# Layer 0 of a two-layer transformer block: the attention scores of two query blocks issued together

## The chip, the cores and the metric

The kernel runs on one core of one Trainium2 chip. The time is the device time of one execution in microseconds, and the median of three runs is compared. All tensors are float32. TensorE (PE) does matmuls and transposes and loads weights beside them (PEld); VectorE (DVE), ScalarE (ACT) and GpSimd (POOL) do the rest; SyncE (SP) issues most DMAs. Matmul results go to PSUM, which has eight banks of 512 float32 values on each of 128 partitions.

## The reference, cut to what matters

Two post-norm layers follow each other: causal attention with 32 heads of 16 dimensions and 8 key/value heads, then a linear layer with dequantized weights; attention with heads of 128 dimensions and a distance bias, then a linear layer with ternary weights. Only the first attention is touched by the change. Four sequences (batches) of 256 tokens:

```
q = (x @ Wq + bq).reshape(B, S, 32, 16).transpose(0, 2, 1, 3)
k = (x @ Wk + bk).reshape(B, S, 8, 16).transpose(0, 2, 1, 3)
v = (x @ Wv + bv).reshape(B, S, 8, 16).transpose(0, 2, 1, 3)
...
scores = jnp.einsum('bhqd,bhkd->bhqk', q, k) / jnp.sqrt(16.)
scores = jnp.where(causal, scores, NEG)
p = jax.nn.softmax(scores, axis=-1)
out = jnp.einsum('bhqk,bhkd->bhqd', p, v)
...
x = _layernorm(x + out @ Wo + bo)
```

## The kernel before, in words

The attention of layer 0 is a loop of 64 steps (L584 to L594): batch b (0 to 3), query tile qt (0 or 1, 128 tokens each), parity e of the key/value head (0 or 1), and block n (0 to 3) of 32 queries. A step is one call of `begin0`. Its four score matmuls (L502) take the four key/value heads of one parity, one in each quarter of 32 rows of the PE array; a block's four query heads times 32 queries are the 128 columns of the weights, and the keys are streamed. Causality lets a step stop at w = 128 qt + 32 (n + 1) keys, so the width runs over 32, 64, 96 and 128 in the first tile and 160, 192, 224 and 256 in the second. Each matmul writes its own bank: the tile `sc` has four banks, and its pool `ps_s0` holds one such tile. The other four banks are three for everything else (`ps_w`) and one for the attention's result `o`.

DVE adds the mask and moves the scores to SBUF in one instruction (L505: pr <- sc, causal), which is what frees the four banks. It takes the maximum (L511: nm); ACT does four exponentials with their sums (L289); DVE takes the reciprocal of the sums of the block before (L294, in `divided`, kept in program order), and POOL multiplies by it (L297). Six `pr` buffers rotate. Four steps later `transpose0` turns the probabilities on PE (L535: pt), and ACT or DVE copies them to `prT0` (L107, L105: prT). After the fourth block of a parity `end0` multiplies by v (L551: o). After both parities `o` is copied to `oT`, and a generator `tail0` for that 128-token tile starts: py = oT @ Wo (L458), residual and statistics (y L460, L272 to L274), a power on POOL (rs L275), normalisation (x L279), four transposes (pt_x L285), a copy to x1T (L107), the second matmul pf (L475), again norm, transposes and a copy to x2T. `fill` advances these tails and the projections of the next batch (`project0`: pk L401, pq L414, pv L434) by one piece a step.

The order in which instructions stand on an engine is not written out by hand: the tile framework reorders the program by its own estimates, apart from instructions that are kept in program order. Each engine runs its list in order, so an instruction that waits holds up everything behind it. In the second tile most copies of prT, and the copy of oT, are ACT's, in the same list as the exponentials (L566 gives the second tile's copies to ACT).

The norm of batch b, tile qt is called with tt = 2 b + qt. Where the text says "batch 1, pf to py", it means pf of tile tt = 1, whose matmuls run while batch 1 is in the attention, and py of tt = 2.

Of the kernel before, what the change touches and what calls it, by code (L numbers as in the profile page):

```python
# [12 lines left out]
F32 = mybir.dt.float32  # L13
# [7 lines left out]
P = 128  # L21
# [43 lines left out]
def block_kernel(  # L65
# [20 lines left out]
    nc = tc.nc  # L86

    def pool(stack, name, bufs=1, **kw):
        return stack.enter_context(tc.tile_pool(name=name, bufs=bufs, **kw))
# [42 lines left out]
    for g in range(G - 1):  # L132
        rows = slice(32 * g, 32 * g + 32)
# [8 lines left out]
    ps_s0 = pool(la, "ps_s0", 1, space=PSUM)  # L142
# [145 lines left out]
    def exponentials(pr, sc, nm, sums, i, w):  # L288
        nc.scalar.activation(  # L289
            pr[:, i, 0:w], sc, AF.Exp, bias=nm[:, i : i + 1], accum_out=sums[:, i : i + 1]  # L290
        )
# [9 lines left out]
    def softmax_tiles(sp, name, bufs, room=True):  # L301
        nm = sp.tile([P, G], F32, tag="nm", name=f"nm_{name}", bufs=bufs + 2)
        sums = sp.tile([P, G], F32, tag="sums", name=f"sums_{name}", bufs=bufs + 2)
        pr = sp.tile([P, G, 2 * P], F32, tag="pr", name=f"pr_{name}", bufs=bufs) if room else None
        return nm, sums, pr
# [69 lines left out]
    qkv0 = {}  # L375
# [114 lines left out]

    ahead, tails = deque(), deque()

    def begin0(b, qt, e, n):

        qT, kT, _ = qkv0[b]
        w = qt * P + 32 * (n + 1)
        name = f"0_{b}_{qt}_{e}_{n}"
        nm, sums, pr = softmax_tiles(a0, name, 6)
        sc = ps_s0.tile([P, 4, 4 * P], F32, tag="s", name=f"sc_{name}")
        for r in range(4):  # L500
            rows = slice(32 * r, 32 * r + 32)
            nc.tensor.matmul(  # L502
                sc[:, r, 0:w], qT[rows, 4 * qt + n].rearrange("p i q -> p (i q)"), kT[rows, e, 0:w], start=True, stop=True
            )
        nc.vector.tensor_tensor(  # L505
            pr[:, :, 0:w],
            sc[:, :, 0:w],
            causal[:, 2 * P - w :].unsqueeze(1).to_broadcast([P, G, w]),
            ALU.add,
        )  # L510
        nc.vector.tensor_reduce(nm, pr[:, :, 0:w], AX.X, ALU.max, negate=True)  # L511
        for r in range(4):
            exponentials(pr, pr[:, r, 0:w], nm, sums, r, w)
        divide0()
        undivided.append((pr, sums, w))
        return pr

    open0 = {}
    undivided = []

    def divide0():


        if undivided:
            divided(*undivided.pop(), True)
# [52 lines left out]
    def fill():  # L578
# [5 lines left out]
    run(  # L584
        [(b, qt, e, n) for b in range(B) for qt in range(2) for e in range(2) for n in range(4)],
        begin0,
        transpose0,
        end0,
# [543 lines left out]
```

## Time and profile before

| | us |
|---|---|
| median of three runs (936.08 to 938.96) | 937.45 |
| the profiled execution | 938.1 |
| its span, first to last instruction | 936.3 |
| PE busy | 894.2 (95%) |
| DVE busy | 600.0 (64%) |
| POOL busy | 427.8 (46%) |
| ACT busy | 315.6 (34%) |
| the attention of layer 0 with its tails, from the trace | about 20 to 250 |

The first row is what is compared. The profiled execution is one more execution, with 1.8 us outside its span. A busy share is of the whole span, and the two layers differ: ACT is far busier in layer 0 than its 34% says. A row of a timeline gives start, duration, engine, line, what is written and read, the shape, how many records it merges, and in brackets the idle time before it and what ended it. A matmul of float32 leaves two records, a transpose one. Stretches are given as A:B, with length, then busy time and instructions of PE, PEld, DVE, ACT and POOL, then the granted PE clock, the DMA share and GB/s.

### The profile page before, as it was taken

How to read it: one execution, taken by the hardware profiler on the slowest of the kernel's cores; microseconds unless marked ns; L12 is line 12 of the kernel's file. 1: busy time of each engine (PE TensorE's matmuls, PEld its weight loads, DVE VectorE, ACT ScalarE, POOL GpSimd, SP SyncE). 2: the span in 40 equal slices, each digit the busy share in tenths (PEclk: the TensorE clock that was granted, in tenths of full speed). 3: DMA queues.
4: the chain of work that ended last, by engine and by line, in shares of the span. 5: the costliest groups of instructions: out<-in, count | busy, mean ns of one | idle time of the engine just before them, and what ended most of it. 6: DMA issues, size and time to landing. Idle time of an engine off the chain costs nothing.

```text
span 936.3 us, 12053 instructions
## 1 busy us (share of the span) xinstructions
PE 894.2 (95%) x3849; PEld 549.0 (59%) x3849; DVE 600.0 (64%) x1393; ACT 315.6 (34%) x1220; POOL 427.8 (46%) x470
## 2 busy tenths in 40 slices
PE   7989999998999998999999999999999999999995
PEld 6655565554444445666666666666666666667552
DVE  2867867868324457555676676666676666666575
ACT  1675675668410012222212222122221121214341
POOL 4443543435355124336434634543553534657732
PEclk9999999999999999999999999999999999999998
DMA  9500000000110104434443544353444433432001
GB/s 251 186 1 1 1 2 1 1 1 1 44 48 22 45 1 105 121 102 142 106 134 82 134 134 113 112 135 93 122 123 113 121 84 111 135 90 71 1 34 57
DMA packets 76421, 74.49 MB, mean 80 GB/s; under 512 B 5957, under 2 KB 52678, under 8 KB 76358
## 3 DMA queue, kind: packets, MB, share of 16 engines
q1 hardware_dynamic: 75014, 72.02, 27.0%
q10 hardware_dynamic: 1344, 1.70, 0.6%
q8 instruction: 31, 0.51, 0.2%
q14 instruction: 32, 0.26, 0.1%
HBM read 49.58 MB, written 24.12 MB: 79 GB/s over the span
## 4 chain that ended last, share of the span: by engine, by line
PE 80%; POOL 7%; DVE 7%; ACT 3%; issue 1%; DMA 1%; ACTq 0%; POOLq 0%; DVEq 0%
PE p_q L658 19%; PE po L911 15%; PE o L1037 8%; PE sc L999 7%; PE p_k L658 5%; PE p_v L658 5%; PE py L458 3%; PE pf L475 3%; PE py L868 3%; PE pq L414 2%; PE pt L535 2%; ACT pr L289 2%; PE o L551 2%; PE sc L502 2%; POOL pr L297 1%; DVE pr L505 1%
## 5 line engine op out<-in xcount | busy, mean ns | idle before, releaser
L297 POOL TENSOR_TENSOR pr<-pr,sums 128x512 f32<-128x512 f32 (+7 forms) x128 | 168.6, 1318 | 230.7 <-DVE sums L294 214.3
L289 ACT ACTIVATE pr<-sc,nm 128x32 f32<-128x32 f32 (+7 forms) x256 | 95.0, 378 | 236.3 <-DVE nm L1015 214.3
L289 ACT ACTIVATE pr<-pr,nm 128x32 f32<-128x32 f32 (+7 forms) x256 | 102.9, 403 | 45.8 <-DVE sums L294 28.2
L1007 DVE SCALAR_TENSOR_TENSOR sc<-table,sc 128x224 f32<-128x224 f32 (+7 forms) x256 | 87.7, 364 | 27.5 <-PE sc L999 25.7
L999 PEld LDWEIGHTS sc<-kT,qT 128*128 128x128 f32 x512 | 77.1, 191 | 32.6 <-issue 29.2
L1037 PE MATMUL o<-prT,v 128*128 128x512 f32 x192 | 92.9, 592 | 0.0
L672 DVE TENSOR_TENSOR qT<-p_q,qT 128x512 f32<-128x512 f32 x96 | 64.8, 687 | 37.3 <-PE p_q L658 37.3
L999 PE MATMUL sc<-kT,qT 128*128 128x160 f32 (+7 forms) x512 | 84.9, 307 | 1.9 <-ACT pr L289 1.9
L1015 DVE TENSOR_REDUCE nm<-sc 128x1 f32<-128x224 f32 (+7 forms) x256 | 71.3, 300 | 2.7
L323 DVE STREAM_TRANSPOSE blocks<-pr 128x512 f32<-128x512 f32 x84 | 57.3, 697 | 24.4 <-POOL pr L297 24.3
L911 PE MATMUL po<-wo,so 128*128 128x256 f32 x224 | 57.9, 381 | 2.6 <-POOL so L635 2.6
L658 PE MATMUL p_q<-x2T,ws_q 128*128 128x512 f32 x128 | 59.8, 592 | 0.0
L658 PE MATMUL p_q<-xt,ws_q 128*128 128x512 f32 x128 | 58.1, 595 | 0.0
L658 PE MATMUL p_q<-x2T,wq 128*128 128x512 f32 x128 | 57.6, 592 | 0.0
L107 ACT COPY o<-o 128x512 f32<-128x512 f32 x29 | 17.0, 585 | 120.4 <-PE o L1037 120.4
L911 PE MATMUL po<-wo,o 128*128 128x256 f32 x224 | 57.5, 379 | 0.0
L911 PE MATMUL po<-to,so 128*128 128x256 f32 x224 | 54.7, 388 | 0.9 <-POOL so L638 0.9
L107 ACT COPY prT<-pt 128x512 f32<-128x512 f32 (+2 forms) x82 | 44.4, 579 | 33.0 <-PE pt L535 28.7
L505 DVE TENSOR_TENSOR pr<-sc,causal 128x128 f32<-128x128 f32 (+3 forms) x64 | 47.6, 744 | 12.4 <-PE sc L502 11.6
L535 PE MATMUL pt<-ident,pr 128*128 128x128 f32 (+3 forms) x384 | 53.1, 275 | 2.2 <-ACT prT L107 1.9
L924 DVE TENSOR_TENSOR kept<-po,kept 128x512 f32<-128x512 f32 x48 | 33.1, 689 | 31.6 <-PE po L911 31.6
L911 PEld LDWEIGHTS po<-to,so 128*128 128x128 f32 x224 | 42.9, 193 | 16.6 <-issue 9.1
(165 smaller groups left out, 1541.6 us busy)
## 6 DMA issues: line engine op xcount, KB each, us to landing
way<-blocks SPq DMA_DIRECT2D x112, 128.0 KB, 2.5
prT<-way SPq DMA_DIRECT2D x28, 512.0 KB, 3.7
wq<-in_L_attn_w_qkv_dram SPq DMA_DIRECT2D x8, 1024.0 KB, 5.2
wo<-in_L_attn_w_o_dram SPq DMA_DIRECT2D x8, 1024.0 KB, 5.3
way<-blocks SPq DMA_DIRECT2D x112, 64.0 KB, 1.8
prT<-way SPq DMA_DIRECT2D x28, 256.0 KB, 2.6
wk<-in_L_attn_w_qkv_dram SPq DMA_DIRECT2D x4, 512.0 KB, 3.8
wv<-in_L_attn_w_qkv_dram SPq DMA_DIRECT2D x2, 1024.0 KB, 6.2
```

Source lines behind the costliest of these rows:

```text
L107: nc.scalar.copy(dst, src)
L289: nc.scalar.activation(pr[:, i, 0:w], sc, AF.Exp, bias=nm[:, i : i + 1], accum_out=sums[:, i : i + 1])
L297: nc.gpsimd.tensor_tensor(pr[:, :, 0:w], pr[:, :, 0:w], sums.unsqueeze(2).to_broadcast([P, G, w]), ALU.mult)
L323: nc.vector.transpose(blocks[:, kt].rearrange("p j h q -> p h j q"), pr[:, :, ts(kt, P)].rearrange("p h (j k) -> p h j k", k=32),)
L535: nc.tensor.transpose(pt[0:w, r, :], pr[:, r, kt * P : kt * P + w], ident)
L658: nc.tensor.matmul(bank, fixed, moving, start=(c == 0), stop=(c == 1))
L672: add = lambda dst, a, b: nc.vector.tensor_tensor(dst, a, b, ALU.add)
L911: nc.tensor.matmul(bank[:, ts(n, HALF)], left[:, c, :], right[:, c, :], start=(c == 0), stop=(c == 1),)
L999: nc.tensor.matmul(sc[:, m, 0:w], qT[:, 8 * b + 4 * qt + n].rearrange("p i q -> p (i q)"), kT[:, b * S : b * S + w], start=True, stop=True,)
L1007: nc.vector.scalar_tensor_tensor(sc[:, m, 0:w], table[:, 2 * P - w : 2 * P], table[:, 2 * P + kv : 2 * P + kv + 1], sc[:, m, 0:w], ALU.mul ...
L1015: nc.vector.tensor_reduce(nm[:, n : n + 1], sc[:, m, 0:w], AX.X, ALU.max, negate=True)
L1037: nc.tensor.matmul(o, v1[:, 2 * b + kt, ts(kv, P)], prT[:, kt].rearrange("p h n q -> p (h n q)"), start=(kt == 0), stop=(kt == qt),)
```

## The change

A new function `scores0` computes the scores of two neighbouring blocks, n and n + 1, when n is even, into one `sc` tile of the same four banks: each bank (512 values) is cut into two halves of 256, one a block. `begin0` calls it at even n only, keeps the tile in `open0`, and takes its half of it at every step. The number of matmuls, their shapes and the number of all other instructions stay as they are; the tile `sc` now comes free when the mask adds of both blocks have read it.

```diff
+    def scores0(b, qt, e, n):
+
+        qT, kT, _ = qkv0[b]
+        sc = ps_s0.tile([P, 4, 2, 2 * P], F32, tag="s", name=f"sc_0_{b}_{qt}_{e}_{n}")
+        for m in range(2):
+            w = qt * P + 32 * (n + m + 1)
+            for r in range(4):
+                rows = slice(32 * r, 32 * r + 32)
+                nc.tensor.matmul(
+                    sc[:, r, m, 0:w],
+                    qT[rows, 4 * qt + n + m].rearrange("p i q -> p (i q)"),
+                    kT[rows, e, 0:w],
+                    start=True,
+                    stop=True,
+                )
+        return sc
+
     def begin0(b, qt, e, n):
 
-        qT, kT, _ = qkv0[b]
         w = qt * P + 32 * (n + 1)
         name = f"0_{b}_{qt}_{e}_{n}"
         nm, sums, pr = softmax_tiles(a0, name, 6)
-        sc = ps_s0.tile([P, 4, 4 * P], F32, tag="s", name=f"sc_{name}")
-        for r in range(4):
-            rows = slice(32 * r, 32 * r + 32)
-            nc.tensor.matmul(
-                sc[:, r, 0:w], qT[rows, 4 * qt + n].rearrange("p i q -> p (i q)"), kT[rows, e, 0:w], start=True, stop=True
-            )
+        if n % 2 == 0:
+            open0["sc"] = scores0(b, qt, e, n)
+        sc = open0["sc"][:, :, n % 2]
         nc.vector.tensor_tensor(
             pr[:, :, 0:w],
             sc[:, :, 0:w],
```

## The prediction

> **What bounds the kernel now.** I read the page first, then busy time by stretches, the timeline of the first layer engine by engine, the waits of the score matmuls, and last the granted clock window by window. The change touches layer 0's attention alone (20 to 250 us), so the table by stretches matters most. Its columns are PE, PEld, DVE, ACT and POOL busy, PEclk, DMA share, GB/s; the cuts are batch ends, roughly.
>
> ```profile
> 20.00:60.00 40.00, 34.37 (x291) 24.56 (x290) 31.98 (x65) 30.10 (x127) 17.33 (x16) 1.00 0.38 131
> 60.00:118.00 58.00, 54.14 (x359) 32.26 (x357) 42.94 (x83) 35.25 (x141) 25.50 (x25) 0.97 0.00 1
> 118.00:177.00 59.00, 55.94 (x384) 34.35 (x384) 43.70 (x88) 37.09 (x149) 25.59 (x26) 1.00 0.00 1
> 177.00:229.00 52.00, 47.99 (x337) 26.38 (x338) 40.43 (x81) 36.79 (x149) 22.27 (x22) 1.00 0.01 1
> ```
>
> PE is busy 92 to 95% of three of the four, so it is the usual bound. But DVE and ACT have 60 to 80%, and PE's idle time is not spread: it stands before a few matmuls that wait for the softmax. The waits say which:
>
> ```profile
> L502 PE MATMUL sc<-kT,qT x512: 270/333/479, 21.3 to 233.5; 32*128 32x32 f32 x22, 32*128 32x128 f32 x22, 32*128 32x192 f32 x22, 32*128 32x64 f32 x21
> its engine sat idle before it (us, times) until:
>   DVE pr L505: 25.3, 32
> ...
>   DVE pr L505: 11.6, 15
> ```
>
> The first 25.3 us is PE (and its weight loader, counted beside it) waiting for the mask add L505 to free the four banks; the 11.6 us is DVE waiting for scores. Next the place that decides the sum, batch 1, second query tile (timeline of PE, then ACT):
>
> ```profile
> 111.06 0.55 PE L502 MATMUL sc<-kT,qT 32*128 32x160 f32 x8
> ...
> 113.84 0.61 PE L502 MATMUL sc<-kT,qT 32*128 32x192 f32 x8 [1.09 <-DVE pr L505]
> ...
> 116.28 0.66 PE L502 MATMUL sc<-kT,qT 32*128 32x224 f32 x8
> 117.97 1.55 PE L458 MATMUL py<-wop,oT 128*128 128x512 f32 x3 [1.02 <-ACT oT L107]
> ...
> 116.39 1.04 ACT L107 COPY prT<-pt 128x512 f32<-128x512 f32 x2
> 117.33 0.58 ACT L107 COPY oT<-o 128x512 f32<-128x512 f32 x1
> 117.81 0.46 ACT L289 ACTIVATE pr<-pr,nm 128x192 f32<-128x192 f32 x1
> ```
>
> PE sits twice: for L505, and for ACT's copy oT, which stands behind one block's exponentials. Last, the clock around the two worst PE waits:
>
> ```profile
> 56.86:60.27 3.41, 1.67 (x12) 0.68 (x10) 2.26 (x3) 3.38 (x13) 1.02 (x2) 1.00 0.02 5
> 60.27:63.69 3.42, 3.42 (x6) 1.36 (x5) 0.00 (x0) 1.34 (x6) 1.00 (x1) 0.50 0.00 0
> 111.47:114.89 3.42, 2.33 (x28) 1.75 (x23) 3.29 (x5) 1.50 (x4) 1.32 (x3) 1.00 0.00 0
> 114.89:118.30 3.41, 2.39 (x22) 0.97 (x20) 3.03 (x5) 3.41 (x14) 3.12 (x2) 1.00 0.01 2
> ```
>
> A window with PE busy 1.67 of 3.41 us is followed by one at half clock; 2.33 and 2.39 are not punished (nor 1.91 at 855.6 us). 1.70 at 370.9 is. So the point lies at about 1.7 us idle, and one half-clock window costs up to 1.7 us of PE work.
>
> **The Trainium skill.** "TensorEngine Tiling (Array Packing)", Key Properties: changing the tiling mode drains TensorE. The trace agrees, priced below. "TensorE: Matmul & The Clock Gate", Part 1: the clock halves after an idle window of 3413 ns that runs free. The trace has this length, but half a window idle is enough. "PSUM — Partial Sum Buffer", section "PSUM bank collisions raise a hardware error": TensorE may not write a bank that another engine reads. So the first add cannot start while the second block's scores enter the same banks; no run here shows that case.
>
> **What a switch costs.** Scores use a quarter of the rows each (32*128), transposes the whole array. Transposes follow each other every 0.109 us, from row 132.49 in the timeline of 120 to 134 us: 12 take 1.46 to the next start, of which the first is 0.06 and the last 0.09 us too long. Between them a score group takes 0.35 us at width 32 and 0.64 at 256 (126.36 to 126.72, 124.26 to 124.90). So one w=256 group costs 0.79 with both edges; merged behind another it adds only its two streams, 2 x 0.215 (py: eight 512-column matmuls in 3.44 us, half of it for 256): 0.36 saved. At width 32/64 weight loads of 0.107 show and 0.29 is saved. The instruction orders give 68 runs of score matmuls before and 37 after (five pairs are split), and 157 changes of mode against 102. 31 runs x 0.33 = 10 us, which I use as 0.17 per saved change, 55 of them, 9.4 us. Matmul count, DMAs, SP's order and all of layer 1's order are the same, so nothing else is removed.
>
> **What moves.** (1) Scores of block n+1 are issued a step early, and the wait for L505 comes once per pair. (2) On DVE both adds now stand ahead of the first maximum: the first block's exponentials start one add later (0.81 to 1.21 us; row 128x768 is 0.93). (3) On ACT's order, in the second tile of batches 1, 2, 3, oT stands behind the exponentials of two blocks instead of one, and the x1T copy that pf needs likewise. A block of 192 is 4 x 0.445 = 1.78 us. (4) The added self-waits of PE name matmuls 9 or more back (once 5), which are over: nothing; if not, 0.1 us each (an edge as above), 22 of them. (5) POOL has the power that the norm needs behind one division more (up to 1.7 us) at the end of first tiles; L297 is done by then because the exponentials are earlier; else 1.7 us, where PE has other work.
>
> **The sum**, as lead (-) or lag (+) against the profiled run at the matmuls py and pf:
> - Batch 0, to py (59.67): ACT is busy from 41 us on and sets the end. It loses about 0.8 us waiting for the late maximum, gains 0.6 from earlier scores: +0.2.
> - To pf of tile 1 (105.27): of the waits of 1.7 us at 72.94, 75, 76 and 88, 1.5 go, since the adds are through before; with 8 changes (1.3 us) and 0.5 waiting for x1T, -2.1.
> - Batch 1, pf to py: now 12.70 us. After: +0.93 (second add) +1.78 (second exponentials) -0.94 (the two prT copies leave this chain): 14.4. -2.1 + 1.7 = -0.4. PE's own work there (pf 3.44, pq 1.7, 20 transposes 2.2, o 1.1, two score pairs 2.0) is 10.5 us: it idles 3.9 us in one piece, over the 1.7 point wherever the window falls. Half clock: +1.4 (0.7 to 1.7 by phase): +1.0.
> - Batch 2: 13 changes, -2.2, and the waits at 157.89 and 146.47, -1.1: -2.3; then again +1.7 and +1.4: +0.8.
> - Batch 3, to pf (216.16): 8 changes and a wait of 0.3, -1.7: -0.9 at py; its chain is 14.3 (3.7 from py to y, 4.0 statistics and norm, 1.7 two adds, 0.8 maximum, 3.45 two exponentials, 0.6 x1T) against 12.1: +2.2, so +1.3. Clock on pf itself +1.4: +2.7.
> - pf to py (228.65): 13.7 (3.6 to y, 3.6 to the norm, 1.7 adds, 0.8 maximum, 3.4 exponentials, 0.6 oT) against 12.5, +1.2; then 2.1 back, since the last block's scores are already done (0.9), the division before 240.59 is early (0.9) and two changes go (0.3); half clock once more +1.4: 3.2.
> From 250 us on nothing differs. The profiled execution took 938.1 us (span 936.3), 0.65 above the median 937.45. 937.45 + 3.2 is 940.7; I say 940.8, 0.36% slower. What measures apart from no change is about 0.3%, 2.8 us.
>
> **Rivals.** (A) Faster: the oT and x1T delays find cover, PE's waits before py stay under 1.7 us, no window halves. It then keeps the 9.4 us, less some 1 us at batch 0: about 929. For: PE is busy over 92%. Against: ACT's order puts eight exponentials before oT, and no PE work is left there. It decides at an idle of 1.7 us per window: below it, this; above, mine. With half of the chain's delay, 933. (B) Chains as computed, but the clock holds: four times 1.4 us less, 935.1, no change. Against: both half-idle windows of the trace were punished. (C) Larger stalls: DVE's reciprocals wait for exponentials in program order, so each delay blocks the adds behind them, a further 1 us per second tile and one more halving: 946. (D) The change does nothing, as all scores wait for the same adds: 937.5; the order, with 31 runs fewer, speaks against it.
>
> **Numbers.** Mine 0.46 (938.5 to 944), C 0.08, A 0.30, B 0.13, D 0.03. Mine falls partly within 0.3% (0.05). Faster 0.31, same 0.2, slower 0.49. The range leaves out the best of A and the worst of C: 929.5 to 945.5. Both signs hold much; the likeliest case's own range is 938.5 to 944.
>
> **What would show it.** Right: score rows x16, L505 mean unchanged, PE waiting for scores under 8 us against 25.3; PE idle of 3 us or more before py in batches 1 to 3 <-ACT oT; more than one window at 0.50 between 60 and 250 us. Wrong: oT waits under 1.5 us (A), or clock at 1.00 throughout (B); a wait for L505 over 2 us at each pair (C).

## The result and the profile after

The changed kernel takes 945.13 us (median of five runs, 942.64 to 947.94), the kernel before 936.32 in the same comparison. The ratio is 1.0096 (95% interval 1.0081 to 1.0111): 8.8 us slower. The direction was forecast, the size was not: 3.3 us were expected. The profiled execution of the changed kernel is its longest run, 947.94 us with a span of 946.1, against 938.1 and 936.3 before; its excess of 9.8 us is the one taken apart here. Below, py_2 is the py of tile tt = 2, and so on.

The same four stretches as before the change (length, then busy time of PE, PEld, DVE, ACT, POOL, granted clock):

```profile
20.00:60.00 40.00, 33.30 (x295) 25.18 (x294) 32.99 (x67) 31.09 (x132) 18.62 (x16) 0.96 0.41 132
60.00:118.00 58.00, 53.22 (x365) 32.58 (x364) 41.17 (x83) 35.37 (x144) 24.77 (x25) 0.97 0.00 1
118.00:177.00 59.00, 54.22 (x384) 34.52 (x383) 43.63 (x88) 37.16 (x149) 25.87 (x25) 0.97 0.01 2
177.00:229.00 52.00, 45.81 (x332) 26.59 (x335) 36.35 (x77) 32.92 (x131) 19.77 (x20) 0.94 0.00 1
```

PE is busy less in every stretch, and yet gets no further: its clock, 1.00 in three of the four before, is now 0.94 to 0.97 in all. A busy share that falls can mean that work was saved or that the engine waits; here it is both. What the score matmuls wait for (the waits of their line, 502 before, 501 now):

```profile
L501 PE MATMUL sc<-kT,qT x512: 270/318/478, 21.5 to 229.0; 32*128 32x64 f32 x22, 32*128 32x128 f32 x22, 32*128 32x192 f32 x22, 32*128 32x32 f32 x21
...
  DVE pr L518: 8.6, 8
...
  DVE pr L518: 9.9, 7
```

PE's wait for the mask add fell from 25.3 us in 32 places to 8.6 in 8, and DVE's wait for scores from 11.6 to 9.9. The change does what it says (the forecast had put the first wait under 8). Now the place shown before, batch 1, second tile (timeline of PE, then of ACT):

```profile
112.46 1.09 PE L501 MATMUL sc<-kT,qT 32*128 32x224 f32 x16
117.19 2.66 PE L458 MATMUL py<-wop,oT 128*128 128x512 f32 x4 [3.64 <-ACT oT L107]
...
113.16 0.43 ACT L289 ACTIVATE pr<-pr,nm 128x160 f32<-128x160 f32 x1 [0.89 <-DVE sums L294]
...
114.82 0.44 ACT L289 ACTIVATE pr<-pr,nm 128x192 f32<-128x192 f32 x1
...
116.57 0.56 ACT L107 COPY oT<-o 128x512 f32<-128x512 f32 x1
```

The wait for oT before py is 3.64 us in one piece, where it was 1.02: eight exponentials, of 160 and of 192 columns, stand ahead of the copy instead of four. The o that it copies was finished at 112.5. Batches 2 and 3 have the same wait (3.64 and 3.70 us), and so has batch 0, for which the forecast named none: its py_0 starts at 58.40, after PE has waited 3.66 us for ACT's copy oT. Two of the five places where the clock is halved, each with the window ahead of it (PE busy is the first figure after the length; the clock is the figure after POOL's count):

```profile
173.00:176.39 3.39, 0.00 (x0) 0.00 (x0) 2.43 (x4) 3.39 (x16) 2.82 (x2) 1.00 0.00 0
176.39:179.80 3.41, 3.23 (x4) 1.51 (x5) 2.40 (x4) 2.23 (x10) 1.47 (x1) 0.50 0.00 0
...
227.60:231.00 3.40, 1.09 (x16) 0.69 (x16) 2.44 (x6) 1.92 (x9) 1.78 (x1) 1.00 0.00 0
231.00:234.42 3.42, 1.31 (x2) 0.79 (x3) 3.42 (x6) 2.24 (x10) 1.38 (x3) 0.50 0.00 0
234.42:237.83 3.41, 3.41 (x5) 1.34 (x5) 0.92 (x1) 1.79 (x8) 1.45 (x1) 0.50 0.00 0
```

In batch 2 one whole window passes with PE idle. In batch 3 the wait for oT straddles two windows, and the clock stays at half for 6.83 us. Between 20 and 260 us the clock is at half for 23.9 us in five pieces (from 56.92, 118.36, 176.39, 217.35 and 231.00), against one piece of 3.41 us before.

The books, from the first score matmul to the first matmul of py_7, which closes layer 0. PE counts as busy while it or its weight loader runs; half of the busy time inside a halved window is booked as lost to the clock; what remains is work at full clock, with the edges at changes of the tiling mode in it. The columns are worked out from the records of the profiled executions.

| us | length | idle | lost to clock | work | after py_7 to the end: length (lost to clock) |
|---|---|---|---|---|---|
| before | 228.1 | 18.7 | 1.7 | 207.7 | 686.9 (1.7) |
| changed | 235.9 | 29.1 | 9.9 | 196.8 | 688.7 (2.7) |
| difference | +7.8 | +10.4 | +8.2 | -10.9 | +1.8 (+1.0) |

So the saving is there in full, 10.9 us of work. It was paid back nearly twice: 10.4 us of new waits and 8.2 us of clock that, as experiment six shows, the waits cost.

### The profile page after: what moved, and what is told of

It is laid out like the page before. It is cut to its first block, busy times and chain, and to the rows that moved or that the text cites. A ratio compares the mean times of both kernels' runs of the same rounds, so it can differ in the third digit from the quotient of the medians.

```text
span 946.1 us, 12065 instructions
## 1 busy us (share of the span) xinstructions
PE 892.1 (94%) x3849; PEld 551.2 (58%) x3849; DVE 596.1 (63%) x1393; ACT 315.5 (33%) x1220; POOL 428.4 (45%) x470
## 4 chain that ended last, share of the span: by engine, by line
PE 79%; POOL 7%; DVE 6%; ACT 5%; DMA 1%; issue 1%; SPq 0%; ACTq 0%; POOLq 0%; DVEq 0%
PE p_q L671 19%; PE po L924 15%; PE o L1050 8%; PE sc L1012 7%; PE p_k L671 5%; PE p_v L671 5%; PE py L458 4%; ACT pr L289 3%; PE pf L475 3%; PE py L881 3%; PE pq L414 2%; PE pt L548 2%; PE o L564 2%; DVE pr L518 1%; POOL pr L297 1%; POOL to L910 1%
## 5 line engine op out<-in xcount | busy, mean ns | idle before, releaser
L289 ACT ACTIVATE pr<-sc,nm 128x32 f32<-128x32 f32 (+7 forms) x256 | 95.2, 378 | 233.9 <-DVE nm L1028 220.8
L458 PE MATMUL py<-wop,oT 128*128 128x512 f32 x64 | 37.9, 747 | 15.6 <-ACT oT L107 15.3
L518 DVE TENSOR_TENSOR pr<-sc,causal 128x128 f32<-128x128 f32 (+3 forms) x64 | 45.5, 745 | 10.5 <-PE sc L501 9.9
```

The costliest lines, as they stand in the source:

```text
L289: nc.scalar.activation(pr[:, i, 0:w], sc, AF.Exp, bias=nm[:, i : i + 1], accum_out=sums[:, i : i + 1])
L458: nc.tensor.matmul(py, oT[:, i, :], wop[:, i, :], start=(i == 0), stop=(i == G - 1))
```

## The experiments

All were compared with the kernel before on the same chip; its median was 936.57, 936.0 and 936.4 in the three groups (first to fourth, fifth to eighth, ninth and tenth), each on another chip. Where a trace is read, it is that of one execution.

**One: the second add behind the first maximum.** Against the changed kernel, in `begin0`:

```diff
+        with tc.issue_after(open0["max"]) if n % 2 else nullcontext():
             nc.vector.tensor_tensor(pr[:, :, 0:w], sc[:, :, 0:w], ...)
-        nc.vector.tensor_reduce(nm, pr[:, :, 0:w], AX.X, ALU.max, negate=True)
+        most = nc.vector.tensor_reduce(nm, pr[:, :, 0:w], AX.X, ALU.max, negate=True)
+        open0["max"] = most.ins
```

> Score pairs as in the changed kernel, but the second block's mask add is issued behind the first block's maximum. Theory S (serial softmax chain: the loss is the later start of the first block's exponentials plus oT and x1T behind two blocks of exponentials, plus halved clock windows that the stalls bring): the exponentials start some 0.9 us earlier and x1T is ahead of the second block again in batches 2 and 3, oT is still behind both blocks; PE's stalls before py of batches 1 to 3 shrink from 3.65 to about 2.7 us, one halved window goes: 941 us (938 to 944), DVE waits unchanged. Rival W (the pairing itself costs: PE has to wait for both adds of a pair before it may write either half, whatever the order behind it): 945 or, as the second add is later now, up to 948.

Measured: 934.69 us, ratio 0.9982 (0.9972 to 0.9992). Theory S is right in direction, and the gain of 10.4 us is more than twice what it asked for. The stalls before py of batches 1 to 3 are 2.53 us, close to the 2.7 expected, but at py_2 and py_4 that won nothing: pf_1 to py_2 takes 14.26 us as against 14.22, since the scores now wait 1.17 us for the second add of the pair before. The gain lies at two other places. The stall of 3.66 us before py_0, which the forecast had not named, and its two halved windows are gone, which makes first score to pf_1 6.2 us shorter; the x1T stall of 2.7 us before pf_5 and its halved window are gone too, 4.0 us from py_5 to py_6. The books (idle 21.9 us, lost to clock 6.4, first score to py_7 11.0 us shorter than in the changed kernel) are those of the fastest of 22 runs, 931.99 us. Rival W, by which the pairing itself costs, is out as the cause of the loss: the pairs are all there, and PE's waits for adds even rose, from 8.6 to 13.6 us.

**Two: oT ahead of the second block's exponentials.** Against the changed kernel, for one block of each of batches 1 to 3:

```diff
-        for r in range(4):
-            exponentials(pr, pr[:, r, 0:w], nm, sums, r, w)
+        open0["exp"] = lambda: [exponentials(pr, pr[:, r, 0:w], nm, sums, r, w) for r in range(4)]
+        if not (b and (qt, e, n) == (1, 1, 1)):
+            open0.pop("exp")()
...
+    def late0():
+        if "exp" in open0:
+            with tc.issue_after(open0["oT"].ins):
+                open0.pop("exp")()
```

> The changed kernel, with only the exponentials of one block (batch 1 to 3, second tile, e=1, n=1) issued behind the copy oT. Theory S: each of three stalls before py falls from 3.65 to about 1.9 us, the x1T stall of batch 3 (2.7 us) stays; most of the halved windows before py go: 945.1 - 3 x 1.8 - about 3 of clock = 937 us (934 to 940). Rival W: 945, as PE's score waits are untouched. Rival N (the exponentials that are put back become the next bound: the adds and divisions behind them come 1.8 us later each): 942 to 945, with PE waiting for sc or pt instead of oT.

Measured: 938.36 us, ratio 1.0009 (0.9996 to 1.0022), not to be told from the kernel before and 6.8 us under the changed one. The stalls before py are 1.88, 1.88 and 1.95 us; the 2.70 us before pf_5 stays, as does the 3.66 us before py_0, which this edit does not touch, and so do halved windows from 55.9, 209.4 and 223.1. PE has no new wait of over 0.9 us behind the exponentials that were put back, so rival N is out.

**Three: both orders put back.** The two edits above together, the score pairs untouched.

> Score pairs as in the changed kernel, with both orders put back: second add behind the first maximum, and that one block's exponentials behind oT. Theory S: stalls before py of 1.0 us or less as before the change, no halved window at py of batches 1 to 3, the 9 us of mode switches are kept: 929 us (927 to 932), faster than the kernel before by 0.8%. Rival W: 945. Rival N: 936 to 940, the gain is taken by waits for sc and pt.

Measured: 924.36 us, ratio 0.9866 (0.9844 to 0.9888): 12.2 us faster than the kernel before, and better than S asked for. This is a version that beats both kernels. The same place as above (PE, then ACT):

```profile
106.60 1.09 PE L501 MATMUL sc<-kT,qT 32*128 32x224 f32 x16 [1.17 <-DVE pr L519]
108.47 1.98 PE L458 MATMUL py<-wop,oT 128*128 128x512 f32 x4 [0.78 <-ACT oT L107]
...
106.96 0.41 ACT L289 ACTIVATE pr<-pr,nm 128x160 f32<-128x160 f32 x1
107.37 0.56 ACT L107 COPY prT<-pt 64x512 f32<-64x512 f32 x1
107.84 0.58 ACT L107 COPY oT<-o 128x512 f32<-128x512 f32 x1
108.31 0.46 ACT L289 ACTIVATE pr<-pr,nm 128x192 f32<-128x192 f32 x1
```

The wait for oT is 0.78 us. A wait of the scores for the second add of the pair before them (1.17 us) has come back, but the clock is at 1.00 through the whole of layer 0 in this execution. In the books: idle 17.7, lost to clock 0, work 196.1; 213.8 us from first score to py_7 against 228.1. Of the 14.3 us that are gone 11.7 are work, 1.7 clock and 1.0 idle, so the gain is the work that the pairs save. The two orders alone, without pairs, were not run; the kernel before has them already: adds and maxima alternate in all of its 64 steps, as here, and its oT is ahead of the second block's exponentials.

**Four: the kernel before, with oT alone made late.** No pairs here; one added edge on ACT:

```diff
             oT = a0.tile([P, G, P], F32, tag="oT", name=f"oT0_{b}_{qt}")
-            evacuate(oT.rearrange("p i q -> p (i q)"), o)
+            with tc.issue_after(open0["exp"]) if b and qt == 0 else nullcontext():
+                evacuate(oT.rearrange("p i q -> p (i q)"), o)
```

> The kernel before (one block of scores at a time, no pairs), with only the copy oT of the first tiles of batches 1 to 3 issued behind the next block's exponentials. Theory S: each py comes up to 1.8 us later and PE's stall there rises from about 1.0 to 2.8 us, so a halved window of 1.7 us joins it: 936.3 + 3 x (1.8 + 1.7) = 946.8 at most, 941 to 947 with what other work covers. Rival W: 936.3, within 0.3%, since no pair is there. Halved windows between 60 and 250 us: 3 or more by S, 1 by W.

Measured: 948.44 us, ratio 1.0121 (1.0094 to 1.0147), just above the expected band. Putting three copies of 0.57 us behind four exponentials each costs 11.9 us in a kernel that has no pairs at all. Batch 1 (PE, then ACT):

```profile
119.45 2.84 PE L458 MATMUL py<-wop,oT 128*128 128x512 f32 x6 [2.78 <-ACT oT L107]
...
118.83 0.57 ACT L107 COPY oT<-o 128x512 f32<-128x512 f32 x1
```

The waits before py_2 and py_4 are 2.78 and 2.79 us and set the program back by 1.8 us each, as S has it; yet neither was followed by a halved window: the first gave PE 1.78 us idle in one window, the second was cut in two by a boundary. In batch 3 the delay moved to waits for L505 (1.91 and 1.39 us ahead of py_6), and those did halve the clock, for 6.8 us from 233.7: another 2.8 to py_6 and 1.8 on to pf_6. A last 1.8 us fell behind py_7, where one more window was halved than in the kernel before. Of the three or more halved windows that S named between 60 and 250 us only these two came, beside the one near 60 us that the kernel before has too. That a copy behind four exponentials costs its py 1.8 us is shown; that the clock follows each such stall is not.

**Five: the last block's exponentials first.** In the changed kernel, ACT's order near 240 us (batch 3), where the forecast had given time back (PE around it, then ACT, the changed kernel):

```profile
233.11 6.03 PE L458 MATMUL py<-wop,oT 128*128 128x512 f32 x8 [3.70 <-ACT oT L107]
...
243.26 1.59 PE L548 MATMUL pt<-ident,pr 128*128 128x128 f32 x12 [1.81 <-ACT x2T L107]
...
239.61 1.07 ACT L107 COPY prT<-pt 128x512 f32<-128x512 f32 x2 [3.40 <-PE pt L548]
240.57 0.52 ACT L289 ACTIVATE pr<-pr,nm 128x256 f32<-128x256 f32 x1
```

ACT idles 3.40 us for transposes that stand behind the slow py, with four ready exponentials queued behind the copy. The edit traces the last two blocks together and moves that one group:

```diff
+            with tc.issue_after(open0["last"]) if (b, qt, e, n) == (3, 1, 0, 2) else nullcontext():
+                evacuate(prT[...], pt[...])
```

> The changed kernel with one move on ACT and none elsewhere: the last block's exponentials (batch 3, second tile, e=1, n=3) stand ahead of the two prT copies that wait for transposes behind py_6. Theory Q (at the end of layer 0 the forecast gave 2.1 us back and the chip did not, because those exponentials, ready at 235.3 us, stand in ACT's queue behind copies that wait for a py at half clock): they run from 236.0 instead of 240.6, PE's stall of 1.8 us at 243 goes to 0.5 or less, py_6 to py_7 falls from 24.3 to about 22.6 us: 943.4 us (942 to 944.3). Rival P (what is late there is the norm: POOL's power stands behind a division of 1.7 us, and that order is untouched): 945 and the same 24.3 us.

Measured: 942.41 us, ratio 1.0072 (1.0057 to 1.0086). Q is right: the stall is gone, and py_6 to py_7 takes 22.42 us.

**Six: filler on PE in the stalls.**

```diff
+        if tt in (2, 4, 6):
+            with tc.issue_after(open0["pair"]):
+                for _ in range(3):
+                    nc.tensor.matmul(py, ident, wop[:, 0, :], start=True, stop=True)
```

> The changed kernel with three extra matmuls of 128x512 (0.86 us each, results overwritten) on PE behind the score pair and ahead of py in batches 1, 2 and 3: 2.6 us of the 3.65 us in which PE idles there become busy. Theory K (halved windows are a cost of their own beside the waits): no halved window before py_2, py_4, py_6, and py runs in 3.7 us; three windows' 1.7, 1.6 and 2.4 us come back: 939.4 us (937.5 to 941.5). Rival H (the chain over ACT and DVE sets the pace there, a faster py only waits elsewhere): 944 to 946. If the fillers stand late and push py back: above 946.

Measured: 937.12 us, ratio 1.0006 (0.9995 to 1.0017). The nine added matmuls compute nothing that is kept, the books show 7.7 us more PE work, and the kernel is 8.0 us faster for them. In the trace (PE, batch 1):

```profile
113.11 2.84 PE L460 MATMUL py<-wop,ident 128*128 128x512 f32 x6
116.82 3.70 PE L462 MATMUL py<-wop,oT 128*128 128x512 f32 x8 [0.87 <-ACT oT L107]
```

py starts as late after the scores as ever, but runs at full clock in all three batches; lost to clock is 4.3 us instead of 9.9. That is 5.6 of the 7.6 us by which first score to py_7 is shorter; most of the rest is the idle time from py_6 to pf_6, 1.8 us in the changed kernel and 0.4 here, since the transposes behind a quick py come in time. In the traces a further 1.8 us lie behind py_7, where one window is halved instead of two. This is the cleanest proof that the clock is a cost of its own: the waits' causes were left in place.

**Seven and nine: the same repair in the version with both orders back.** In its trace a stall of 1.7 us is left near 220.8. Seven adds the edit of five; nine also puts the last maximum ahead of y_6 on DVE.

> The version with both orders put back, plus the last block's exponentials ahead of the two prT copies. In its trace PE stalls 1.7 us at 220.8 for a prT copy behind those exponentials. Theory Q: the stall falls under 0.6 us: 923.2 us. Rival P: 924.4, no change, as the norm of tile 6 sets the end.

> The version with both orders put back, plus, for the last block of batch 3 only: its maximum stands ahead of y_6 on DVE and its exponentials ahead of the prT copies on ACT. Theory R (putting the exponentials first alone moved the stall at the end, because their maximum stood behind y_6, which waits for py_6): the maximum is done 1.1 us earlier (216.8 in the clock of the version with both orders back), exponentials run directly behind those of the block before, the division of 896 columns is ahead of the power; PE's stall of 1.7 us before pt goes under 0.5, first score to py_7 falls from 213.8 to 212.2 us: 922.8 us (921 to 924.3). Rival P (the stall is the room of the pt banks, whatever ACT's order): 924.4 or more and a stall of 1.7 us.

Measured: 926.49 us, ratio 0.9899 (0.9885 to 0.9913), and 924.64 us, ratio 0.9877 (0.9855 to 0.9899). Neither is shown to beat 924.36. Seven keeps a stall of 1.72 us; nine cuts it to 1.41, not to 0.5, and first score to py_7 is 215.4 us, not 212.2, in its slowest run of six; of this, 1.7 us are a halved window. Q and R fail here: in all three versions the four exponentials of 256 columns stand right ahead of copies of prT that PE waits for, and the edits only change which copies these are. What would remove this stall stays open.

**Eight and ten: pairs in some batches only.** The pair is taken where `b < 3`, and where `b == 3`:

```diff
-        if n % 2 == 0:
-            open0["sc"] = scores0(b, qt, e, n)
-        sc = open0["sc"][:, :, n % 2]
+        if b < 3:
+            if n % 2 == 0:
+                open0["sc"] = scores0(b, qt, e, n, 2)
+            sc = open0["sc"][:, :, n % 2]
+        else:
+            sc = scores0(b, qt, e, n, 1)[:, :, 0]
```

> The changed kernel with pairs in batches 0 to 2 only; batch 3 takes one block of scores at a time as before. Theory S: the traces put py_5 0.6 us ahead of the kernel before and all of the lag behind it, so without batch 3's pairs the time is 936.3 - 0.6 and some clock, 936 us (934.5 to 938). Rival E (every batch loses alike, some 2.2 us each, and the lead at py_5 is chance): 942 to 944.

> The changed kernel with pairs in batch 3 only. Theory S with the loss placed in batch 3: the complement of the version without batch 3's pairs (938.0), so 936.3 + 8.8 - 1.7 = 943.4 us (942 to 945), PE idle before pf_5 2.7 and before py_6 3.7 us. Rival (the loss in batch 3 needs the halves of earlier batches, or is chance of the clock's windows): 937 to 940.

Measured: 938.03 us, ratio 1.0031 (1.0017 to 1.0045), just above the band, and 946.22 us, ratio 1.0104 (1.0089 to 1.0119), above the band. Batch 3 alone costs as much as all four do (the intervals of 9.8 and 8.8 us overlap). The two losses, 2.0 and 9.8 us, sum to more than 8.8: with pairs in batch 3 only, pf_5 and py_6 each fall into halved windows of 6.8 us (6.2 us lost there), where the changed kernel loses 1.6 and 2.4. Same stalls (2.70 and 3.70 us), other positions relative to the windows. That most of the loss comes with batch 3's pairs is shown; the sum over places is not additive.

## Why the prediction was wrong, by its own steps

Lead (-) or lag (+) of the profiled executions at the forecast's own marks:

| at | forecast | measured | |
|---|---|---|---|
| py_0 | +0.2 | -1.3 | from the first score 1.5 us sooner: 2.6 us of work less, 1.1 us more idle |
| pf_1 | -2.1 | -2.3 | |
| py_2 | +1.0 | -0.8 | of the forecast, 1.4 is clock, which falls after py starts: +0.4 at pf_2 |
| pf_3 | -2.3 | -2.2 | |
| py_4 | +0.8 | -0.7 | the same: -0.4 at pf_4 |
| py_5 | -0.9 | -0.6 | |
| pf_5 | +1.3 | +1.5 | |
| py_6 | +3.9 | +4.5 | |
| py_7, end of layer 0 | +3.2 | +8.0 | |
| last instruction | +3.2 | +9.8 | |

**Right.** 31 fewer runs of scores: priced at 9.4 us, 10.9 measured as work (the sum itself took off only 31 of its 55 changes of mode, 8, 13, 8 and 2). Two adds ahead of the maximum and two groups of exponentials ahead of oT: the stalls came in one piece of 3.64, 3.64 and 3.70 us where 3.9 was said, and one, two and three show that they go with this order while the pairs stay; four makes such a wait, 2.78 us, without a pair. The half-idle windows halve the clock, and filler undoes it (six). The self-waits of PE cost nothing that shows; no run singles them out.

**Luck.** Up to py_6 the forecast is off by only 0.6 us because two errors nearly cancel. Without the clock, the changed kernel is 1.4 us ahead there, where the sum had 0.3; the start up to py_0, put at +0.2 because ACT was to set its end, is alone 1.5 us better than the sum. The clock had taken 5.9 us more than before, where the sum had 4.2, the largest part of it at py_0, for which the sum had no stall of its own.

**Wrong: "then 2.1 back".** From py_6 to py_7 the sum had +1.4 of clock and -2.1 of earlier work. The same two stretches, end of py_6 to pf_6, before and then changed:

```profile
232.19:241.49 9.30, 8.41 (x73) 5.69 (x72) 4.88 (x9) 8.07 (x25) 4.06 (x4) 1.00 0.01 2
```

```profile
238.97:249.53 10.56, 8.75 (x66) 5.49 (x64) 2.39 (x7) 7.14 (x19) 4.71 (x4) 1.00 0.01 2
```

10.56 against 9.30: +1.3 us instead of -2.1. The scores of the last block did leave this stretch (-0.65). But the wait of 0.9 that was to vanish became 1.8 (+0.9; the second row stands under experiment five):

```profile
240.59 1.06 PE L535 MATMUL pt<-ident,pr 128*128 128x128 f32 x8 [0.89 <-ACT prT L107]
```

It grew since exponentials that were ready sat in ACT's queue behind copies for transposes behind a slow py; five shows that: moving them brings 1.9 us back. And the scheduler split the sixteen records of o into 2 and 14, with four transposes between: 2 took 0.98 us and 14 took 1.85, where 16 in one run took 1.86 (+1.0). The forecast took PE's work to shrink and never asked what ACT would do while py ran at half speed. That term is 3.4 us of the miss.

**Mis-sized: "half clock once more +1.4".** One halved window was priced at 1.4 us, up to 1.7, for each stall. Py_2, py_4 and pf_5 took 1.7, 1.6 and 1.6, but a stall that straddles two windows halves both: py_6 took 6.03 us instead of 3.70, +2.3. This adds 0.9 at this place, and at py_0, where two windows were halved against one before, another 1.0 that the better start there hides. Layer 0 lost 8.2 us more to the clock than before, against 5.6 forecast.

**Wrong: "from 250 us on nothing differs".** Instructions and their order don't differ, and the work after py_7 is 667.3 and 667.2 us (667.1 to 667.6 in all twelve profiles). But in these two executions the windows of the clock lie at the same places to within 0.1 us, while the program is 8.0 us later, so a stall in layer 1 meets other boundaries. Before and then changed:

```profile
370.90:374.30 3.40, 1.69 (x7) 1.11 (x7) 1.04 (x2) 1.24 (x3) 2.52 (x4) 1.00 0.67 155
374.30:377.71 3.41, 3.41 (x9) 2.38 (x8) 0.00 (x0) 1.61 (x7) 0.29 (x1) 0.50 0.49 116
```

```profile
374.36:377.77 3.41, 1.82 (x10) 1.45 (x11) 3.23 (x12) 1.35 (x8) 0.92 (x1) 1.00 0.36 73
377.77:381.18 3.41, 2.40 (x3) 0.35 (x2) 2.17 (x7) 0.59 (x1) 0.43 (x2) 0.50 0.33 99
381.18:384.60 3.42, 2.96 (x7) 2.42 (x8) 0.00 (x0) 0.85 (x3) 2.50 (x4) 0.50 0.62 135
```

One halved window became two: 1.0 us of clock, and 0.9 more of waits behind it, +1.8 in this execution. Over the twelve profiles layer 1's loss to the clock runs from 0 to 4.4 us, with no trend by kernel (0 in experiment one, 4.4 in experiment seven), so it looks like a matter of position and not of the change. That the changed kernel's runs spread over 5.3 us, and that the median excess (8.8) lies below that of the profiled run (9.8), fits with it, but was not traced run by run.

The three terms, 3.4, 0.9 and 1.8, make the forecast's 3.2 into 9.3; the 0.6 already open at py_6 closes it to within 0.1 of 9.8. **Rivals:** A (929) needed cover for oT, which the two orders put back in experiment three supply by hand: 924.4, lower than A said, since 11.7 us of work went instead of 9.4 and the 1.7 us of clock that the kernel before loses at py_0 went too. B is refuted by the halved windows. C had the size (946) largely for other reasons: the stalls in batches 1 to 3 were no longer than forecast, and the additional cost lay in more halved windows, of which C named one, and at the end. D is refuted by the waits.

## What to carry to other kernels

A change that gives the busiest engine less to do also reorders what its helpers do, and a framework's order by estimates may put a short copy that everything waits for behind work that nobody waits for yet. After such a change read each engine's list around the few copies that feed the next long matmul, and pin those; here two pins turned 0.96% slower into 1.3% faster. A stall on PE has to be priced with its clock: count idle time by window, and if a stall can straddle a boundary, price two halved windows, and expect later stalls to meet other boundaries than before.

## What the runs showed of the hardware beyond that

**The two thresholds of the clock.** The Trainium skill, "TensorE: Matmul & The Clock Gate", Part 1, has a free-running window of 3413 ns, the clock at half after an idle one and at full after a busy one; the traces agree on the length (halved stretches inside the program last 3.41 or 6.83 us) and on free-running (the first boundary behind the first score comes 0.03 to 2.19 us after it, at another place in each profile). How idle is idle, over the twelve profiles (PE and loader together): a window at full clock with up to 1.51 us idle was never followed by a halved one, one with 1.80 or more always, and between them it went either way (16 of 28 halved; 1.52 and 1.53 among them, 1.69 and 1.78 not). A window already at half needs much less to stay there: with 0.47 us idle or less the next was full 45 times of 46, with 0.61 or more it was half 14 times of 14. So PE must be almost never idle in a halved window to leave it, which is why stalls that straddle are so dear. What decides in the band from 1.52 to 1.79 us stays open.

**A bank shared by two blocks.** "PSUM — Partial Sum Buffer", section "PSUM bank collisions raise a hardware error", made one expect a delay of the first add while the second block's scores enter the same banks. The adds do start after all sixteen records of the pair, but DVE's waits for scores fell (9.9 us against 11.6), so no cost of it shows here.

**The start.** The first score matmul came at 18.3 to 21.5 us in the twelve profiles, with the same instructions ahead of it in all; times of layer 0 are better compared from there than from the start of the span.
